# A message-passing layer on one core: index transfers spread over stage 1, one add for a group, sums of two groups in one bank, and 39 in place of 53 groups copied by hand

## The chip, the cores and the metric

The kernel runs on one core of one Trainium2 chip. The time is the device time of one execution in microseconds (us); a profile of one further execution gives what each engine did. TensorE is called PE (PEld is its loading of weights), VectorE DVE, ScalarE ACT, GpSimd POOL and SyncE SP in the profile.

## The reference, cut to what matters

There are 12,500 nodes with 128 features and 400,000 edges, sorted by their destination.

```
h   = relu(layernorm(x))
m   = relu(concat(h[src], h[dst], edge_attr) @ w1 + b1) @ w2 + b2
agg = segment_sum(m, dst)
out = x + GRU(agg, h)          # gates r, z, n from agg @ w_ih and h @ w_hh
```

As w1 has 288 rows, the first product splits into three: A = h @ w1[0:128] for the source, B = h @ w1[128:256] + b1 for the destination, and the edge part with the last 32 rows. The product with w2 is taken after the sum over edges.

## The kernel before

**Tiles, units, groups.** 128 edges make a tile, eight tiles (two halves of four) a group. There are 3,125 tiles and 391 groups, the first of them with five tiles. A half group is a unit `u`; the main loop (L1004) runs over 782 units. The order of the work on each engine is that of the program, written out by hand: what stands ahead in an engine's list must be done first.

**Stage 1** (L247 to L379) loops over 26 chunks of up to four tiles of 128 nodes. It loads x in batches of eight tiles (`load`, L263, five buffers), takes mean and variance on VectorE (`bn`, L187), normalises on ScalarE (`relu_norm`, L241), transposes on PE (L337) into `hT_all`, which keeps h transposed in SBUF, multiplies by the first part of w1 (L370), copies the result (`asb`, L346; three of four copies on VectorE) and stores it as table A in DRAM (L365). Ahead of the loop stand, on SyncE's queue, the loads of the first five batches, the weights, and 53 index rows `at` (L310 to L312), one for each group that is copied by hand. Behind the loop stand the stores of the statistics (L376) and the set-up of offsets and windows on VectorE (L398 to L496).

**Gathers.** `gather(k)` (L144) issues eight indirect DMAs on GpSimd for a group, each of 128 rows of A (or, for the first `RAW` = 10 groups, of x) into one of `GBUFS` = 12 tiles `G`. Rows of x are normalised and transposed again in the main loop (`raw_stats`, `raw_h`, `raw_turn`, L607 to L631).

**Groups by hand.** 53 groups are not gathered. For each, an engine copies 1,024 columns of `hT_all`, one edge at a time, at an address read into a register from `at` (`one_by_one`, L897): 26 groups on ScalarE (L909) and 27 on VectorE (L916, two edges at a time, and L921). PE multiplies these columns by the first part of w1 (L655). `SPREAD` (L55) gives the numbers, L90 to L98 spread the groups over the loop, and `run_jobs` (L937) cuts the copying into steps among the other work.

**The main loop.** `stages(u)` (L969) works ahead. `onehot_T` (L538) and `onehot` (L579) make the one-hot rows of the destinations within a window of 32 nodes. `pre(u)` (L636) multiplies one-hot rows and edge features (`L`) by a window of B and the edge part of w1 (`RW`, loaded by `window_rows`, L562) into a bank of PSUM. `add(u)` (L659) adds the gathered rows and takes the relu in one VectorE instruction (L668), for each unit, into one of four tiles `RB`; for a group by hand ScalarE takes the relu (L675). `seg(u)` (L679) sums the edges of a window with the one-hot matrix, one bank of PSUM for each group, which a product with zeros starts (L683). `take` (L692) copies a group's sums to SBUF. Every 14 groups make a block of up to 512 nodes, for which `node(b)` (L738) runs the GRU in steps spread over the next block's units; the last block has its own order (L802). Parts of B, 512 nodes each, are made in the main loop (`batch_product`, L216) at every 16th group, 32 groups ahead.

Of the kernel before, what the change touches and what calls it, by code (L numbers as in the profile page):

```python
# [11 lines left out]
I32 = mybir.dt.int32  # L12
# [23 lines left out]
BLOCKS = [(BP * b, BP, BW) for b in range(26)] + [(364, 10, 384), (374, 9, 352), (383, 8, 320)]  # L36
# [8 lines left out]
RAW = 10  # L45
GBUFS = 12
BATCH = 512
AHEAD = 32
ROOM = V * (AHEAD - 4)
# [5 lines left out]
SPREAD = {"dve": 27, "act": 26}  # L55
START = {"dve": 16, "act": 4}
# [6 lines left out]
def tile_gnn(ctx: ExitStack, tc: tile.TileContext, x, src, srcT, dstT, dstP, eaT, eaP, w1, b1, w2T, b2,  # L63
# [13 lines left out]
    wide = [ps1.tile([128, 512], F32, name=f"wide{i}") for i in range(2)]  # L77
# [35 lines left out]
    def dst_tile(c):  # L113
        if c >= NPL:
# [14 lines left out]
                   allow_small_or_imprecise_dtypes=True)  # L129
    A = dram.tile([N, D], F32, name="A")  # L130
# [29 lines left out]
    RB = [const.tile([128, GRP, D + 4], F32, name=f"RB{i}") for i in range(4)]  # L160
# [55 lines left out]
    def batch_product(j, pm, pool, name, bufs):  # L216
# [3 lines left out]
        rows = min(BATCH, N - n0)  # L220
        for i in range(0, rows, 128):
            m = min(128, rows - i)
            nc.tensor.matmul(pm[:m, i:i + D], hT_all[:, n0 + i:n0 + i + m], w1b, start=True, stop=True)
# [19 lines left out]


    st_all = const.tile([128, NT, 2], F32, name="st_all")
    nc.vector.memset(st_all[:, NFULL, :], 0.0)
    with tc.tile_pool(name="pp", bufs=3) as pp:  # L247
# [62 lines left out]
        for r in range(NJ):  # L310
            t0 = tiles(by_hand[r])[0]
            nc.sync.dma_start(at[r:r + 1, :], row(src[t0 * 128:(t0 + PAIR) * 128]))  # L312
# [13 lines left out]
        NC = len(chunks)  # L326
        for q in range(NC + 3):
# [5 lines left out]
            if 1 <= q <= NC:  # L333
                b, i0, c, e, P, n0 = chunk(q - 1)
                pts[q - 1] = wide[q % 2]
                for j in range(c, e):
                    nc.tensor.transpose(pts[q - 1][:, (j - c) * P:(j - c + 1) * P],  # L337
                                        xs[b][:P, j, :], ident[:P, :P])
                if e == bats[b][1]:
                    load(b + 5)  # L340
            if q >= 3:
# [3 lines left out]
                copy = nc.scalar.copy if q % 4 == 2 else nc.vector.tensor_copy  # L345
                copy(asb[b][:P, c:e, :], pas.pop(q - 3)[:P, :e - c, :])  # L346
# [11 lines left out]
            if q in (6, 8):  # L358
                batch_product(q // 2 - 3, ps1.tile([128, 512], F32, name="nd"), pp, "bt", 1)
            if q in (7, 9):  # L360
                batch_store(q // 2 - 3)
# [4 lines left out]
            if 2 <= q <= NC + 1:  # L366
                b, i0, c, e, P, n0 = chunk(q - 2)
                pas[q - 2] = ps2.tile([128, GRP, D], F32, name="pre")
                for j in range(c, e):
                    nc.tensor.matmul(pas[q - 2][:P, j - c, :], columns(b, j, j + 1)[:, 0, :],  # L370
                                     w1a, start=True, stop=True)
        for b0, b1, n in ((0, 1, BAT[0]), (1, 12, 8), (12, 13, BAT[12])):
            i0 = sum(BAT[:b0])
            for b in range(b0, b1):
# [5 lines left out]

    nc.vector.tensor_copy(wide[0][:, D:D + V], iota)
    p3 = ctx.enter_context(tc.tile_pool(name="p3", bufs=3, reuse_waits="tile"))
    TOT = p3.tile([128, 2 * BW - DMIN], F32, name="TOT", bufs=1)
    DEG = p3.tile([34, 2 * BW - DMIN], F32, name="DEG", bufs=1)
    nc.vector.memset(TOT, 0.0)
    nc.vector.memset(DEG, 0.0)
    nc.vector.memset(DEG[32:34, :BW], 1.0)


    dcol = p3.tile([128, BP + 128], F16, name="dcol", bufs=1)  # L390
    nc.vector.memset(dcol, 0.0)
    dlast = p3.tile([128, BLOCKS[-1][1] + 128], F16, name="dlast", bufs=1)
    nc.vector.memset(dlast, 0.0)
    sums = p3.tile([2 * V, BP, D + 1], F32, name="sums", bufs=1)


    base_f = const.tile([1, NP], F32, name="base_f")
    nc.vector.tensor_copy(base_f[:, 1:], base_d)  # L398
    nc.vector.memset(base_f[:, 0:1], 0.0)
    nc.vector.tensor_scalar(base_f, base_f, float(LAST), 0.0, op0=ALU.min, op1=ALU.max)  # L400
    nc.vector.tensor_copy(at_f[64:65, 512:512 + NP], base_f)
    nc.vector.tensor_tensor(at_f[64:65, :NP], at_f[64:65, 512:512 + NP], at_f[64:65, :NP], op=ALU.is_gt)
    nc.vector.tensor_reduce(beyond, at_f[64:65, :NP], AX.X, ALU.max)
    base_b = p3.tile([128, NP, 2], F32, name="base_b", bufs=1)
    pm = ps1.tile([128, 512], F32, name="misc")
    nc.tensor.matmul(pm[:, :NP], ones, base_f, start=True, stop=True)
    nc.vector.tensor_copy(base_b[:, :, 0], pm[:, :NP])
    nc.vector.tensor_scalar(base_b[:, :, 1], pm[:, :NP], float(SHIFT), None, op0=ALU.add)

    place_c = const.tile([2 * V, 1], F32, name="place_c")  # L410
    nc.gpsimd.iota(place_c, pattern=[[0, 1]], base=0, channel_multiplier=1,
                   allow_small_or_imprecise_dtypes=True)
    node_of = p3.tile([2 * V, NP], F32, name="node_of", bufs=1)
    for a in range(2):
        s = slice(V * a, V * (a + 1))
        nc.vector.tensor_scalar(node_of[s, :], base_b[s, :, a], place_c[s, :], float(-V * a),
                                op0=ALU.add, op1=ALU.add)
    blk_f = const.tile([1, NB], F32, name="blk_f")
    groups = [(0, NW, 0, BP, BW)] + [(b, b + 1) + BLOCKS[b] for b in range(NW, NB)]
    for b0, b1_, k0, n, w in groups:  # L420
        nc.vector.tensor_scalar(blk_f[:, b0:b1_], base_f[:, k0:k0 + (b1_ - b0 - 1) * n + 1:n], float(N - w),
                                None, op0=ALU.min)
    blk_i = const.tile([1, NB], I32, name="blk_i")
    nc.vector.tensor_copy(blk_i, blk_f)
    off_f = const.tile([1, NB, 16], F32, name="off_f")
    off_i = const.tile([1, NB, 16], I32, name="off_i")
    base_i = const.tile([1, NB, 16], I32, name="base_i")
    step_f = const.tile([1, NB], F32, name="step_f")
    step_i = const.tile([1, NB], I32, name="step_i")
    nc.vector.memset(off_f, 0.0)  # L430
    off_c = p3.tile([128, NB * 16], F32, name="gt", bufs=3)[:1, :].rearrange("o (b n) -> o b n", n=16)
    nc.vector.memset(off_c, 0.0)
    step_c = const.tile([1, NB], F32, name="step_c")
    nc.vector.tensor_tensor(step_f[:, 1:], blk_f[:, 1:], blk_f[:, :-1], op=ALU.subtract)
    nc.vector.memset(step_f[:, 0:1], float(BW))
    for b0, b1_, k0, n, w in groups:
        ks = base_f[:, k0:k0 + (b1_ - b0) * n].rearrange("o (b n) -> o b n", n=n)
        nc.vector.tensor_tensor(off_f[:, b0:b1_, :n], ks,
                                blk_f[:, b0:b1_, None].to_broadcast([1, b1_ - b0, n]), op=ALU.subtract)
        nc.vector.tensor_scalar(base_i[:, b0:b1_, :n], ks, float(4 * D), None, op0=ALU.mult)  # L440
        nc.vector.tensor_scalar(off_c[:, b0:b1_, :n], off_f[:, b0:b1_, :n], float(w - V - SHIFT), 0.0,
                                op0=ALU.min, op1=ALU.max)
    for b0, b1_ in [(0, 1), (1, NW + 1)] + [(b, b + 1) for b in range(NW + 1, NB)]:
        nc.vector.tensor_scalar(step_c[:, b0:b1_], step_f[:, b0:b1_], float(BLOCKS[max(b0 - 1, 0)][2]),
                                float(LEAST[b0]), op0=ALU.min, op1=ALU.max)
    nc.vector.tensor_copy(off_i, off_c)
    nc.vector.tensor_tensor(off_f, off_f, off_c, op=ALU.not_equal)
    nc.vector.tensor_copy(step_i, step_c)
    nc.vector.tensor_tensor(step_f, step_f, step_c, op=ALU.not_equal)
    dloc = const.tile([128, T], F16, name="dloc")  # L450
    lim = const.tile([128, 2, NPL], F32, name="lim")

    def place(c):
        if c >= NPL:
            return
        k0, k1 = c * PLACE, min(NP, (c + 1) * PLACE)
        t0, t1 = tiles(k0)[0], tiles(k1 - 1)[1]
        df = p2.tile([128, CH], F32, name="dst_f")
        nc.vector.tensor_copy(df[:, :t1 - t0], dst_i.pop(c)[:, :t1 - t0])
        if k0 == 0:  # L460
            for a in range(2):
                e = min(SUP0, (a + 1) * GRP)
                nc.vector.tensor_scalar(dloc[:, a * GRP:e], df[:, a * GRP:e],
                                        float(-SHIFT * a), None, op0=ALU.add)
        kb = max(k0, 1)
        tb = tiles(kb)[0]
        nc.vector.tensor_tensor(
            dloc[:, tb:t1].rearrange("p (k t) -> p k t", t=GRP),
            df[:, tb - t0:t1 - t0].rearrange("p (k t) -> p k t", t=GRP),
# [747 lines left out]
```

## Time and profile before

| | us |
|---|---|
| median of three runs | 3459.87 (3456.93 to 3460.8) |
| the profiled execution | 3466.03 |
| its span, first to last instruction | 3464.3 |

The page gives busy time by engine and by group of instructions. Rows of groups read: line, engine, operation, what is written and read, count, then busy time with the mean of one in ns, and behind the second bar the idle time of the engine just ahead of them and what ended most of it. Rows of the timeline read: start, duration, engine, line, operation, and in brackets the idle time before and what ended it ("issue" is time in which the engine waited for nothing that the profile shows). Rows of stretches give start and end, length, the busy time of PE, PEld, DVE, ACT and POOL with their instructions, the granted clock of PE, the busy share of the DMA engines and GB/s. The mean granted clock of PE was 0.796.

### The profile page before, as it was taken

What the parts mean: (1) busy time and instruction counts of PE and PEld (TensorE: products, weight loads), DVE (VectorE), ACT (ScalarE), POOL (GpSimd) and SP (SyncE); (2) the same over time, 40 slices, a digit from 0 to 9 for tenths busy, and PEclk for the clock granted to TensorE, in tenths of its full rate; (3) what the DMA queues carried; (4) which work ended last, traced back from release to release, by engine and by line L of the source; (5) the groups of instructions that cost most, each with busy time, mean ns of one, the idle gap of its engine ahead of it and who ended that gap; (6) DMA issues with size and microseconds to landing.
All of it is one profiled execution on the core that took longest, in us unless ns stands there. A gap on an engine that the chain in (4) does not pass through costs nothing. (4 is left out here: it accounts for less than half of the span.)

```text
span 3464.3 us, 83484 instructions
## 1 busy us (share of the span) xinstructions
PE 2463.0 (71%) x13272; PEld 1569.1 (45%) x13272; DVE 2298.2 (66%) x17007; ACT 2873.0 (83%) x27061; POOL 2596.0 (75%) x2710
## 2 busy tenths in 40 slices
PE   5567767767777776677767776776777667757767
PEld 5444444444444454454444444444444444434445
DVE  6756666666666676666666667666666666666673
ACT  4499798888879897979888889888988986998782
POOL 7577777777777777777777777777777777777776
PEclk8787787867877887777777778786888788888878
DMA  5433333333343333433333343333333433333332
GB/s 189 106 85 90 94 97 97 92 98 94 93 100 100 93 95 95 101 94 92 101 94 95 94 99 96 97 95 95 94 95 97 100 91 94 98 94 95 88 92 72
DMA packets 187723, 336.15 MB, mean 97 GB/s; under 512 B 64727, under 2 KB 108310, under 8 KB 187179
## 3 DMA queue, kind: packets, MB, share of 16 engines
q0 software_dynamic: 86432, 177.19, 21.9%
q1 hardware_dynamic: 100603, 153.54, 16.2%
q14 instruction: 434, 3.56, 0.3%
q8 instruction: 110, 1.80, 0.2%
q10 hardware_dynamic: 144, 0.07, 0.0%
HBM read 310.29 MB, written 20.26 MB: 95 GB/s over the span
## 5 line engine op out<-in xcount | busy, mean ns | idle before, releaser
L152 POOL DMA_INDIRECT G<-A,src_i x2624 | 2521.6, 961 | 826.7 <-issue 755.6
L909 ACT COPY HE_act<-hT_all 128x4 uint8 x26624 | 2683.1, 189 | 65.6 <-issue 42.2
L916 DVE SCALAR_TENSOR_TENSOR both<-hT_all 128x4 uint16 x13824 | 1181.6, 155 | 992.9 <-issue 983.2
L644 PE MATMUL pre<-RW,L 128*128 128x256 f32 x3128 | 1161.6, 499 | 878.1 <-DVE RB L668 839.3
L644 PEld LDWEIGHTS pre<-RW,L 128*128 128x128 f32 x3128 | 669.7, 239 | 1200.2 <-DVE RB L668 965.7
L688 PE MATMUL seg<-RB,OH 128*32 128x129 f32 x6250 | 614.2, 328 | 0.1
L668 DVE CUSTOM_DVE_ANT_0 RB<-pre,G 128x512 f32<-128x512 f32 x656 | 444.1, 677 | 43.4 <-DMA G<-A,src_i 20.2
L688 PEld LDWEIGHTS seg<-RB,OH 128*32 128x32 f32 x6250 | 335.8, 126 | 208.9 <-issue 151.8
L675 ACT ACTIVATE RB<-pre 128x512 f32<-128x512 f32 x126 | 74.3, 589 | 152.1 <-PE pre L655 151.8
L772 ACT ACTIVATE gt<-nd 128x512 f32<-128x512 f32 (+2 forms) x28 | 16.5, 588 | 219.6 <-PE nd L766 219.6
L545 DVE TENSOR_SCALAR L<-L,node_of 64x512 f32<-64x512 int32 x383 | 188.6, 493 | 5.9 <-DMA L<-in_dstP 5.9
L596 DVE TENSOR_TENSOR OH<-dloc,wide 128x256 f32<-128x256 f16 (+1 forms) x392 | 159.6, 407 | 0.5 <-issue 0.5
L713 PE MATMUL nd<-spot,sums 64*128 64x40 f32 x766 | 114.3, 319 | 0.0
L713 PEld LDWEIGHTS nd<-spot,sums 64*128 64x128 f32 x766 | 110.5, 229 | 7.7 <-issue 7.7
L683 PEld LDWEIGHTS <-zrow 1*64 1x64 bf16 x391 | 42.7, 109 | 156.7 <-issue 148.3
L696 DVE COPY sums<-seg 64x129 f32<-64x129 f32 x391 | 108.4, 277 | 3.8 <-PE seg L688 3.8
L683 PE MATMUL seg<-zrow 1*64 1x129 bf16 x391 | 104.1, 266 | 1.0 <-DVE sums L696 1.0
L921 DVE COPY HE_dve<-both 128x512 uint8<-128x512 uint8 x216 | 95.8, 443 | 7.4
L152 POOL DMA_INDIRECT G<-in_x,src_i x77 | 72.9, 946 | 24.5 <-issue 23.2
L655 PEld LDWEIGHTS pre<-w1a,HE_dve 128*128 128x128 f32 x432 | 80.0, 231 | 9.3
L655 PE MATMUL pre<-w1a,HE_dve 128*128 128x128 f32 x432 | 79.6, 316 | 0.0
L655 PEld LDWEIGHTS pre<-w1a,HE_act 128*128 128x128 f32 x416 | 72.1, 217 | 8.0
(193 smaller groups left out, 1395.5 us busy)
## 6 DMA issues: line engine op xcount, KB each, us to landing
L<-in_dstP SPq DMA_DIRECT2D x195, 256.0 KB
L<-in_eaP SPq DMA_DIRECT2D x195, 256.0 KB
G<-A,src_i POOLq DMA_INDIRECT x2624
RW<-B SPq DMA_DIRECT2D x782, 16.0 KB
xb<-in_x SPq DMA_DIRECT2D x26, 256.0 KB
out<-xb SPq DMA_DIRECT2D x26, 256.0 KB
xs<-in_x SPq DMA_DIRECT2D x11, 512.0 KB
A<-asb SPq DMA_DIRECT2D x11, 512.0 KB
```

The source lines that it names most:

```text
L152: nc.gpsimd.indirect_dma_start(out=G[k][:, j, a, :], out_offset=None, in_=table, in_offset=bass.IndirectOffsetOnAxis(ap=src_i[c][:, i:i + ...
L545: nc.vector.tensor_scalar(o, i, node_of[:, k:k + 1], None, op0=ALU.is_equal)
L596: nc.vector.tensor_tensor(o, d.to_broadcast(shape), i.to_broadcast(shape), op=ALU.is_equal)
L644: nc.tensor.matmul(PP[u][:, 2 * i:2 * i + 2, :], Ls[k // QP][:, c0:c0 + 128], RW[k % 4], start=True, stop=not raw)
L655: nc.tensor.matmul(PP[u][:, 2 * i + a, :], cols, w1a, start=False, stop=n + 1 == len(l) or l[n + 1][1] != j)
L668: nc.vector._custom_dve(TENSOR_ADD_SAT, out=RB[u % 4][:, :, :D], in0=PP.pop(u), in1=unit(u), s0=float("inf"), s1=0.0)
L683: nc.tensor.matmul(SEG[k][:2 * V, :D + 1], zrow[:, :2 * V], zrow[:, :D + 1], start=True, stop=False)
L688: nc.tensor.matmul(SEG[k][V * a:V * (a + 1), :D + 1], OH[k][:, j, a, :], RB[u % 4][:, (j % 2) * 2 + a, :D + 1], start=False, stop=all(b != ...
L696: nc.vector.tensor_copy(sums[:, slot(block(k), k - BLOCKS[block(k)][0]), :], pm[:2 * V, :D + 1])
L713: nc.tensor.matmul(p[:, bass.ds(offs[i], V + SHIFT)], sums[:, slot(b, i), :D], spot, start=False, stop=i == len(offs) - 1)
L909: nc.scalar.copy(he[:, e * 4:e * 4 + 4], column(v))
L916: nc.vector.scalar_tensor_tensor(both[:, (e0 % PIECE + i) // 2, :], column(vals[i + 1]), 256.0, column(vals[i]), op0=ALU.mult, op1=ALU.add)
```

## The change

- **Index transfers.** The rows `at`, now 39, are issued three to a chunk of stage 1, from the fifth step on.
- **Groups by hand.** `SPREAD` goes from 27 and 26 to 24 (VectorE) and 15 (ScalarE); with `RAW` = 9, nine groups are gathered from x.
- **One add for a group.** The product of a group's two units goes to one tile of two banks, and one add (or relu) covers it, into one of two `RB` tiles; only the last group's add is in halves.
- **Sums of two groups in one bank**, in different rows, taken by one copy after the second; `spot`, `dcol` and `sums` are laid out for it. The blocks at the end become 10, 8 and 9 groups.
- **Stage 1.** Every copy `asb` out of PSUM is on ScalarE; the set-up of offsets runs as a generator among the chunks; three parts of B in place of two are made there.
- **Later.** Parts of B are 448 nodes (14 windows of 32) and made in a block's node steps, three blocks ahead; constants are set at group 6 and the statistics stored at group 20.

```diff
-BLOCKS = [(BP * b, BP, BW) for b in range(26)] + [(364, 10, 384), (374, 9, 352), (383, 8, 320)]
+BLOCKS = [(BP * b, BP, BW) for b in range(26)] + [(364, 10, 384), (374, 8, 320), (382, 9, 320)]
-RAW = 10
+RAW = 9
-BATCH = 512
-AHEAD = 32
+BATCH = V * BP
+FIRST = 3
-SPREAD = {"dve": 27, "act": 26}
-START = {"dve": 16, "act": 4}
+SPREAD = {"dve": 24, "act": 15}
+START = {"dve": 14, "act": 4}
...
-        lo, hi = START[m] // 2 + 2, NP - {"dve": 9, "act": 6}[m]
+        lo, hi = START[m] // 2 + 2, NP - {"dve": 7, "act": 5}[m]
...
-        for r in range(NJ):
-            t0 = tiles(by_hand[r])[0]
-            nc.sync.dma_start(at[r:r + 1, :], row(src[t0 * 128:(t0 + PAIR) * 128]))
+        rows_left = list(range(NJ))
+
+        def at_row():
+            if rows_left:
+                r = rows_left.pop(0)
+                t0 = tiles(by_hand[r])[0]
+                nc.sync.dma_start(at[r:r + 1, :], row(src[t0 * 128:(t0 + PAIR) * 128]))
...
-                copy = nc.scalar.copy if q % 4 == 2 else nc.vector.tensor_copy
-                copy(asb[b][:P, c:e, :], pas.pop(q - 3)[:P, :e - c, :])
+                nc.scalar.copy(asb[b][:P, c:e, :], pas.pop(q - 3)[:P, :e - c, :])
...
+            if q >= 4:
+                for _ in range(3):
+                    at_row()
+            if q >= 6:
+                next(setting, None)
...
-        PP[u] = ps2.tile([128, GRP, D], F32, name="pre")
+        if h == 0:
+            PP[k] = ps2.tile([128, PAIR, D], F32, name="pre")
+        p = PP[k][:, GRP * h:GRP * h + GRP, :]
...
+        k, h = divmod(u, 2)
+        if h == 0 and k < NP - 1:
+            return
+        c = slice(0, PAIR) if k < NP - 1 else slice(GRP * h, GRP * h + GRP)
+        o, p = RB[k % 2][:, c, :D], PP[k][:, c, :]
...
-            nc.vector._custom_dve(TENSOR_ADD_SAT, out=RB[u % 4][:, :, :D], in0=PP.pop(u), in1=unit(u),
-                                  s0=float("inf"), s1=0.0)
+            nc.vector._custom_dve(TENSOR_ADD_SAT, out=o, in0=p,
+                                  in1=G[k].rearrange("p j a f -> p (j a) f")[:, c, :], s0=float("inf"), s1=0.0)
...
-        if h == 0:
-            SEG[k] = ps2.tile([128, 512], F32, name="seg")
-            nc.tensor.matmul(SEG[k][:2 * V, :D + 1], zrow[:, :2 * V], zrow[:, :D + 1],
-                             start=True, stop=False)
+        p = SEGB[(k // 2) % 2]
+        if h == 0 and k % 2 == 0:
+            nc.tensor.matmul(p[:, :D + 1], zrow[:, :128], zrow[:, :D + 1], start=True, stop=False)
...
-        if k < 0:
+        if k < 0 or (k % 2 == 0 and k < NP - 1):
             return
-        pm = SEG.pop(k)
-        nc.vector.tensor_copy(sums[:, slot(block(k), k - BLOCKS[block(k)][0]), :], pm[:2 * V, :D + 1])
+        b = block(k)
+        n = spots(k).stop
+        nc.vector.tensor_copy(sums[:n, slot(b, k - BLOCKS[b][0]), :], SEGB[(k // 2) % 2][:n, :D + 1])
...
-        yield 4 if b < NW else 1
+        yield 1
+        batch_product(b + FIRST, p3, "xb", 2)
+        yield 2 if b < NW else 1
         nc.sync.dma_start(out[bass.ds(g0, w), :].rearrange("(p i) f -> p i f", i=4), xb)
+        batch_store(b + FIRST)
...
+            if k == 6:
+                late_setup()
+            if k == 20:
+                store_stats()
```

More of the change, by code (lines that the diff above doesn't have):

```diff
@@ L76, in tile_gnn @@
     ps1 = ctx.enter_context(tc.tile_pool(name="ps1", bufs=1, space=bass.MemoryType.PSUM))
-    wide = [ps1.tile([128, 512], F32, name=f"wide{i}") for i in range(2)]
+    SEGB = [ps1.tile([128, 512], F32, name=f"seg{i}") for i in range(2)]
     dram = ctx.enter_context(tc.tile_pool(name="dram", bufs=1, space=bass.MemoryType.DRAM))
@@ L157, in tile_gnn @@
         gather(k)
-    RB = [const.tile([128, GRP, D + 4], F32, name=f"RB{i}") for i in range(4)]
+    RB = [const.tile([128, PAIR, D + 4], F32, name=f"RB{i}") for i in range(2)]
     for r in RB:
@@ L402, in tile_gnn @@
[L402 to L469, printed above, removed]
-            base_b[:, kb:k1, :].rearrange("p k a -> p (k a)")[:, :, None].to_broadcast(
-                [128, 2 * (k1 - kb), GRP]), op=ALU.subtract)
-        nc.vector.tensor_reduce(lim[:, 0, c:c + 1], dloc[:, t0:t1], AX.X, ALU.max)
-        nc.vector.tensor_reduce(lim[:, 1, c:c + 1], dloc[:, t0:t1], AX.X, ALU.min)
@@ L475, in tile_gnn @@
-    place(0)
-    dst_tile(1)
     w2ih = const.tile([128, 3 * D], F32, name="w2ih")
@@ L583, in onehot @@
         OH[k] = OHB[k % len(OHB)]
-        row = wide[0][:, D:D + V]
+        row = SEGB[((k - 3) // 2 + 1) % 2][:, 256:256 + V]
         for a in range(2) if k == 0 else (None,):
@@ L806, in last_node @@
         yield
-        pd = wide[1][:, :w]
+        pd = ps1.tile([128, 512], F32, name="misc")[:, :w]
         zero(pd)
@@ L815, in last_node @@
         h = hT_all[:, bass.ds(gv, w)]
-        pt = wide[0][:, :w]
+        pt = ps1.tile([128, 512], F32, name="nd")[:, :w]
         zero(pt)
-        for i in range(n - 4):
+        for i in range(n - 3):
             sum_of(b, pt, offs, i)
@@ L1024, in other @@
             run_jobs(u, phase)
-            if h == 0 and phase == 1 and batch_due(k):
-                batch_product(batch_due(k), wide[1], p3, "xb", 2)
-            if h == 1 and phase == 1 and batch_due(k):
-                batch_store(batch_due(k))
             if h == 0 and phase == 3:
```

209 lines of the change are left out of this document (148 added, 61 removed).

## The prediction

> **What bounds the kernel now.** I read the page's first and fifth parts, then the view of the gathers' own line, then GpSimd's timeline, because a busy share alone (ScalarE has the highest) doesn't say which engine is never late for a reason of its own.
>
> ```profile
> span 3464.3 us, 83484 instructions
> PE 2463.0 (71%) x13272; PEld 1569.1 (45%) x13272; DVE 2298.2 (66%) x17007; ACT 2873.0 (83%) x27061; POOL 2596.0 (75%) x2710
> L152 POOL DMA_INDIRECT G<-A,src_i x2624 | 2521.6, 961 | 826.7 <-issue 755.6
> L909 ACT COPY HE_act<-hT_all 128x4 uint8 x26624 | 2683.1, 189 | 65.6 <-issue 42.2
> L916 DVE SCALAR_TENSOR_TENSOR both<-hT_all 128x4 uint16 x13824 | 1181.6, 155 | 992.9 <-issue 983.2
> L668 DVE CUSTOM_DVE_ANT_0 RB<-pre,G 128x512 f32<-128x512 f32 x656 | 444.1, 677 | 43.4 <-DMA G<-A,src_i 20.2
> L696 DVE COPY sums<-seg 64x129 f32<-64x129 f32 x391 | 108.4, 277 | 3.8 <-PE seg L688 3.8
> L921 DVE COPY HE_dve<-both 128x512 uint8<-128x512 uint8 x216 | 95.8, 443 | 7.4
> L152 POOL DMA_INDIRECT G<-in_x,src_i x77 | 72.9, 946 | 24.5 <-issue 23.2
> ```
> ```profile
> L152 POOL DMA_INDIRECT G<-A,src_i x2624: 939/944/1700, 107.9 to 3447.0; - x188
> L152 POOL DMA_INDIRECT G<-in_x,src_i x77: 940/944/1099, 3.4 to 98.5; - x77
> ```
> ```profile
> 107.86 0.96 POOL L152 DMA_INDIRECT G<-A,src_i  x1 [8.26 <-DMA stats<-st_all]
> ...
> 134.37 0.94 POOL L152 DMA_INDIRECT G<-A,src_i  x1 [6.39 <-PE misc L629]
> ...
> 148.65 0.94 POOL L152 DMA_INDIRECT G<-A,src_i  x1 [4.56 <-PE misc L629]
> ...
> 242.66 0.94 POOL L152 DMA_INDIRECT G<-A,src_i  x1 [4.17 <-DVE RB L668]
> ...
> 327.13 0.94 POOL L152 DMA_INDIRECT G<-A,src_i  x1 [4.29 <-DVE RB L668]
> ...
> 3447.00 0.94 POOL L152 DMA_INDIRECT G<-A,src_i  x1 [0.30 <-issue]
> ```
>
> The two gather groups together: 2521.6 + 826.7 + 72.9 + 24.5 = 3445.7 us, busy and idle, for 2624 + 77 = 2701 gathers. That is the whole stretch from the first gather (3.4) to the end of the last (3447.94) and nearly the whole span. The 75% on the page is low only because each gather is followed by 0.30 us of "issue", in which it waits for nothing that the profile shows. The timeline holds just five waits that are longer: 8.26, 6.39, 4.56, 4.17 and 4.29, of which 27.67 - 5 x 0.30 = 26.2 us is real waiting. All five lie before 330 us. After that the gathers run without a hole to the end. So **GpSimd's gathers set the end**, at a pitch of (3445.7 - 26.2) / 2701 = 1.266 us, and what follows the last one, 3464.3 - 3447.9 = 16.4 us, is the tail. The chain of waits covers only the last microseconds and says nothing on this.
>
> The pitch seems to be the gather's own. The 77 gathers from x ran before any byte copy of ScalarE or VectorE, and their median is 944 ns, as it is for the 2624 beside the copies. Only the mean (961) is 17 ns above.
>
> **The change part by part.**
>
> *Groups moved back to gathers.* ScalarE's groups fall from 26 to 15 and VectorE's from 27 to 24, so 14 more of the 391 groups are gathered, eight gathers each: +112. The changed kernel's instruction list agrees: 69 + 2744 = 2813. At the pitch above this costs 112 x 1.266 = **+141.8 us**, all of it on the engine that sets the end. I see no work beside which it could lie.
>
> What it frees is off that path. ScalarE loses 11 x 2683.1 / 26 = 1135 us. VectorE loses, for each group, (1181.6 + 95.8) / 27 = 47.3 us of work and 983.2 / 27 = 36.4 us of waits ahead of it: 3 x 83.7 = 251 us.
>
> *One add for a group, sums of two groups in one bank.* VectorE: 656 adds of 0.677 us (444 us) become 342 twice as wide and two halves; bounded by no longer and twice as long, 233 to 464 us; I take 1.2 us each, nearer to twice, 412 us. Copies of sums fall from 391 to 196 of the same width for each partition: -54 us. PE drops 195 of the starting zero products. ScalarE's relus get wider and fewer. All of this lies beside the gathers and I cost it at nothing; if the cover were gone it would still be a gain. Only the later release could cost: a group's add now waits for its second half, so eight gather tiles come free together. With twelve groups of buffers that is half a group's delay of a 12-group store; I take 0 and bound it by one wait like those above, -0 to +4 us.
>
> *Index transfers.* Here is what the changed kernel wins.
>
> ```profile
> 20.08 17.73 SPq L312 DMA_DIRECT2D at<-in_src  x53
> 37.92 0.84 SPq L268 DMA_DIRECT2D xs<-in_x  x2
> 45.80 1.65 DVE L191 BATCH_NORM_STATS2 bn<-xs 128x6 f32<-128x128 f32 x8 [22.94 <-DMA xs<-in_x]
> 70.00:80.00 10.00, 9.48 (x48) 9.01 (x47) 9.73 (x50) 7.92 (x21) 7.56 (x9) 1.00 0.75 251
> 83.62 0.68 DVE L346 COPY asb<-pre 128x512 f32<-128x512 f32 x1
> 84.81 0.59 ACT L346 COPY asb<-pre 128x512 f32<-128x512 f32 x1 [2.51 <-PE pre L370]
> 105.33 0.29 DVE L346 COPY asb<-pre 84x128 f32<-84x128 f32 x1 [0.69 <-DMA A<-asb]
> 108.15 0.35 DVE L398 CAST base_f<-at 1x390 f32<-1x390 int32 x1
> 119.49 0.67 DVE L191 BATCH_NORM_STATS2 bn<-G 128x6 f32<-128x128 f32 x3
> 143.06 1.19 PE L644 MATMUL pre<-RW,L 128*128 128x256 f32 x2 [8.96 <-DMA RW<-B]
> ```
>
> SyncE issues 53 index rows in one go (0.33 us each) with the sixth load of x behind them at 37.92. It lands at 45.80, and all of stage 1 stands still for 22.94 us. With the rows three to a chunk, from the fifth chunk on, that load goes out at about 20 and lands some 4 to 8 us later, so about 20 of the 22.9 us go. What is late next is VectorE itself (9.73 of 10 us in the stretch from 70 to 80, the third of the busy times in its row; PE, the first, has 9.48). There the change takes 18 copies of A's chunks (0.68 us) off VectorE and puts them on ScalarE (0.59 us), and adds the set-up that now stands between 108.15 and 119.49: 12 against 11 us, nothing in sum. ScalarE goes from 7.9 of these 10 us to about 9.5 (some 3.7 chunks in 10 us, three quarters of them with 0.59 us more), so it nearly ties with the others and I add 2 us. A's last copy comes at 105.3 - 20 + 2 = 87 and is stored by about 90. With RAW at 9 the gathers from x, 69 of them, end at 3.4 + 69 x 1.266 = 90.8. The first gather from A then waits 0 to 3 us in place of 8.26.
>
> The next four waits are for buffers that the main loop frees late. It starts 18 us earlier by stage 1; on VectorE the 11 us of set-up go besides, and on SyncE, ahead of the loads of L, the stats stores (14 issues, estimated at 6 us by the 0.33 us of an index row and some waits). That makes 24 to 29 us, while the gathers come at most 8.0, 14.1, 18.3 and 22.2 us earlier at these four (the waits ahead of them, less 0.30 each, added up). So they lose their cause, the last by little. Taken together I leave 2 of the 26.2 us: **-24 us**; bounds -26 and 0.
>
> *Moved pieces.* Stats stores go to group 20 (some 6 us on SyncE, behind which window rows wait that are four groups, some 36 us, ahead), constants to group 6. Parts of B, now 448 nodes, are stored by the end of a block's node steps, at about group 14(b+2), and read from 14(b+3) - 4: ten groups, about 90 us, of slack. Nothing in sum. In the tail the last group's add is still in halves: 0, within 2 us either way.
>
> *Lighter VectorE.* Gathers next to some VectorE work are longer:
>
> ```profile
> 1514.58 0.94 POOL L152 DMA_INDIRECT G<-A,src_i  x1 [0.30 <-issue]
> 1515.38 0.67 DVE L792 TENSOR_TENSOR gt<-gt 128x512 f32<-128x512 f32 x1
> 1515.83 1.21 POOL L152 DMA_INDIRECT G<-A,src_i  x1 [0.30 <-issue]
> ```
>
> With 11% fewer hand copies there I take 1 ns off the pitch: 1.265. The floor is the median, 0.944 + 0.305 of gap = 1.249. The Trainium skill (SBUF — State Buffer, section Who interferes with whom) states that a VectorE tensor_tensor with both inputs in SBUF, or an op in a two-port mode, holds a port pair against GpSimd, while an op with at most one SBUF input outside these modes does not. The trace agrees on the pair above (both inputs in SBUF, 1.21 us against 0.94). By that rule the wider add, with one input in PSUM, does not slow the gathers, and the sum stays.
>
> **Sum**, on the profiled execution: 3.4 + 2813 x 1.265 + 2 + 16.4 = 3580.2, which is +116 on its span of 3464.3. That execution took 3466.03 with what lies around the span, 6.2 above the median of the three timed runs, 3459.87. I put the same difference on the median: **3576 us**, 3.4% slower.
>
> **The rivals.**
>
> 1. *The early waits stay.* If the sixth load still lands late (SyncE, in order, holding it for PE's transposes of the first batch), or the main loop still starts at about 120 because of the stores and the loads of L and RW (row at 143.06), the 24 us come back: 3600. Against it: the load stands ahead of the rows in the new order on SyncE.
>
> 2. *The gathers fall to their floor.* Only some gathers are longer than the median, and one beside L792 took 1.21 us. If the work that VectorE loses were just what stretches them, the pitch would go to 1.249: 3.4 + 3513.4 + 2 + 16.4 = 3535, on the median 3531; half of the way is 3553. Against it: L792 and the other block steps all remain, and of the hand copies 89%. The rule of the Trainium skill quoted above would allow this, as VectorE's hand copies read SBUF twice.
>
> 3. *The consumers become the bound.*
>
> ```profile
> DVE both L916 <- issue: 983.2, 875, 2.6
> ...
> 3449.68 0.69 DVE L668 CUSTOM_DVE_ANT_0 RB<-pre,G 128x512 f32<-128x512 f32 x1 [4.19 <-DMA G<-A,src_i]
> ```
> From the first product (143) to the last add (3449.7) a group took 8.46 us, with VectorE busy or waiting ahead of its hand copies 2298 + 983 = 3281 us. If the shared banks and the two group-wide result tiles chained PE and VectorE so that a group took over (3565 - 118) / 391 = 8.82 us, the gathers would wait for buffers; every 0.1 us above costs 39 us: at 9.0, 3650. Against it: VectorE gets some 337 us lighter (251 + 54 + 32), 0.86 us a group.
>
> 4. *Not slower.* The gather's base pitch itself holds contention from the byte copies on ScalarE, of which 42% go. The place is each gather. It decides at (3464.3 - 3.4 - 2 - 16.4) / 2813 = 1.223 us: 43 ns less for each gather means no change, and 50 ns less means 1.216, so 3442 on the span and 3438 on the median. Against it: the shortest of all gathers is 939 + 300 ns, and the 77 gathers that ran without any byte copies have the same median.
>
> **How the numbers follow.** Forecast (3565 to 3590) 73%; the early waits stay, in part or whole (3590 to 3602), 10%; floor of the pitch in part or whole (3529 to 3565) 8%; consumers (above 3602) 6%; not slower 3%. The range leaves out the consumers, the lower half of the pitch's way and the last rival: 3553 (half of the way to the floor) to 3602 (no early wait removed, 2 us of tail). A change below 0.2% couldn't be told from none by this kernel's measurement. Slower by more than that: 97%; within: 1%; faster: 2%.
>
> **What would show it.** In the changed profile: 2813 gathers at 1.26 to 1.27 us with no hole after 150 us; gathers as the longest wait of VectorE's add and PE's chain in the main loop, ScalarE's share near half; no wait of 20 us for x at stage 1's sixth batch, A's last copy at 84 to 92; the last gather at about 3564 and a tail of 16 us. It is wrong if gathers get shorter than 0.939 us, if GpSimd waits for VectorE's add again and again through the loop, or if stage 1 still ends after 100.

## The result, and the profile after

| | before | after |
|---|---|---|
| median of four runs, us | 3460.34 | 3579.10 |
| range of the runs | 3456.93 to 3464.28 | 3576.96 to 3579.47 |
| ratio (95% interval) | | 1.0341 (1.0328 to 1.0354) |
| profiled execution, us | 3466.03 | 3576.96 |
| its span | 3464.3 | 3575.2 |

The changed kernel is 3.4% slower, 3 us from the forecast of 3576. The page of its profile, the first lines and the groups that answer to those of before:

```profile
span 3575.2 us, 68446 instructions
...
PE 2457.1 (69%) x12857; PEld 1553.7 (43%) x12857; DVE 2118.9 (59%) x14920; ACT 1729.5 (48%) x15729; POOL 2693.8 (75%) x2822
...
L155 POOL DMA_INDIRECT G<-A,src_i x2744 | 2626.4, 957 | 838.1 <-issue 797.8
L947 DVE SCALAR_TENSOR_TENSOR both<-hT_all 128x4 uint16 x12288 | 1051.1, 152 | 1010.7 <-issue 1005.8
L940 ACT COPY HE_act<-hT_all 128x4 uint8 x15360 | 1542.8, 189 | 31.0 <-issue 17.5
...
L718 PE MATMUL seg<-RB,OH 128*32 128x129 f32 x6250 | 627.4, 334 | 632.3 <-DVE RB L695 626.5
...
L695 DVE CUSTOM_DVE_ANT_0 RB<-pre,G 128x1024 f32<-128x1024 f32 (+1 forms) x344 | 417.7, 1214 | 359.2 <-DMA G<-A,src_i 338.6
...
L803 ACT ACTIVATE gt<-nd 128x512 f32<-128x512 f32 (+2 forms) x28 | 16.5, 588 | 811.8 <-PE nd L797 811.8
...
L155 POOL DMA_INDIRECT G<-in_x,src_i x69 | 66.1, 958 | 21.8 <-issue 20.7
```

Every engine but GpSimd does less than before, and the kernel is slower. ScalarE fell from 83% to 48% and VectorE from 66% to 59%, while GpSimd's 2813 gathers took 2626.4 + 838.1 + 66.1 + 21.8 = 3552.4 us, busy and idle, of the 3575.2. The reader sees who is waiting in the last number of three rows: VectorE's add waited 338.6 us for gathers (20.2 before), PE's sums waited 626.5 us for such adds, and ScalarE 811.8 us for products of PE, whose list holds them behind such sums. GpSimd itself, from the timeline, together with the events of stage 1:

```profile
18.29 2.06 SPq L358 DMA_DIRECT2D xs<-in_x  x2
...
20.88 0.87 SPq L406 DMA_DIRECT2D at<-in_src  x3
...
22.57 1.65 DVE L194 BATCH_NORM_STATS2 bn<-xs 128x6 f32<-128x128 f32 x8 [0.89 <-DMA xs<-in_x]
...
89.29 0.26 ACT L441 COPY asb<-pre 84x128 f32<-84x128 f32 x1 [1.07 <-DMA A<-asb]
...
92.23 0.94 POOL L155 DMA_INDIRECT G<-A,src_i  x1 [2.16 <-DMA dst_i<-in_dstT]
...
3553.56 0.94 POOL L155 DMA_INDIRECT G<-A,src_i  x1 [0.30 <-issue]
```

The sixth load of x now goes out while the statistics of the fifth batch are still in work, the wait of 22.94 us for it is 0.89, A's last copy comes at 89.29 in place of 105.33, and the one wait of GpSimd over 0.45 us after its first gather is 2.16 us. From 92 us to 3554.5 there is no other.

### The profile page after: what moved, and what is told of

The parts are those of the page before. It is cut to its first block, busy times and chain, and to the rows that moved or that the text cites. A ratio compares the mean times of both kernels' runs of the same rounds, so it can differ in the third digit from the quotient of the medians.

```text
span 3575.2 us, 68446 instructions
## 1 busy us (share of the span) xinstructions
PE 2457.1 (69%) x12857; PEld 1553.7 (43%) x12857; DVE 2118.9 (59%) x14920; ACT 1729.5 (48%) x15729; POOL 2693.8 (75%) x2822
## 5 line engine op out<-in xcount | busy, mean ns | idle before, releaser
L155 POOL DMA_INDIRECT G<-A,src_i x2744 | 2626.4, 957 | 838.1 <-issue 797.8
L947 DVE SCALAR_TENSOR_TENSOR both<-hT_all 128x4 uint16 x12288 | 1051.1, 152 | 1010.7 <-issue 1005.8
L940 ACT COPY HE_act<-hT_all 128x4 uint8 x15360 | 1542.8, 189 | 31.0 <-issue 17.5
L718 PE MATMUL seg<-RB,OH 128*32 128x129 f32 x6250 | 627.4, 334 | 632.3 <-DVE RB L695 626.5
L695 DVE CUSTOM_DVE_ANT_0 RB<-pre,G 128x1024 f32<-128x1024 f32 (+1 forms) x344 | 417.7, 1214 | 359.2 <-DMA G<-A,src_i 338.6
L803 ACT ACTIVATE gt<-nd 128x512 f32<-128x512 f32 (+2 forms) x28 | 16.5, 588 | 811.8 <-PE nd L797 811.8
L704 ACT ACTIVATE RB<-pre 128x1024 f32<-128x1024 f32 x48 | 49.0, 1020 | 707.0 <-PE pre L678 675.7
L569 DVE TENSOR_SCALAR L<-L,node_of 64x512 f32<-64x512 int32 x382 | 187.5, 491 | 11.0 <-DMA L<-in_dstP 10.4
L713 PE MATMUL seg<-zrow 1*128 1x129 bf16 x196 | 45.0, 230 | 200.0 <-DVE OH L617 196.7
L617 DVE TENSOR_TENSOR OH<-dloc,seg 128x256 f32<-128x256 f16 (+1 forms) x392 | 160.1, 409 | 0.6 <-issue 0.5
L744 PE MATMUL nd<-spot,sums 128*128 128x40 f32 x782 | 132.1, 345 | 2.0 <-DVE sums L727 2.0
L744 PEld LDWEIGHTS nd<-spot,sums 128*128 128x128 f32 x782 | 127.3, 257 | 12.6 <-issue 10.2
L952 DVE COPY HE_dve<-both 128x512 uint8<-128x512 uint8 x192 | 87.0, 453 | 6.6
L155 POOL DMA_INDIRECT G<-in_x,src_i x69 | 66.1, 958 | 21.8 <-issue 20.7
L793 PE MATMUL misc<-DEG,brow 34*128 34x512 f32 (+2 forms) x112 | 69.2, 701 | 14.8 <-DVE gt L807 14.6
```

What stands on the lines that cost most here:

```text
L155: nc.gpsimd.indirect_dma_start(out=G[k][:, j, a, :], out_offset=None, in_=table, in_offset=bass.IndirectOffsetOnAxis(ap=src_i[c][:, i:i + ...
L569: nc.vector.tensor_scalar(o, i, node_of[:, k:k + 1], None, op0=ALU.is_equal)
L617: nc.vector.tensor_tensor(o, d.to_broadcast(shape), i.to_broadcast(shape), op=ALU.is_equal)
L695: nc.vector._custom_dve(TENSOR_ADD_SAT, out=o, in0=p, in1=G[k].rearrange("p j a f -> p (j a) f")[:, c, :], s0=float("inf"), s1=0.0)
L718: nc.tensor.matmul(p[r0:r0 + V, :D + 1], OH[k][:, j, a, :], RB[k % 2][:, 2 * j + a, :D + 1], start=False, stop=all(b != a for _, _, b in r ...
L744: nc.tensor.matmul(p[:, bass.ds(offs[i], V + SHIFT)], sums[:, slot(b, i), :D], spot[:, i % 2, :], start=False, stop=i == len(offs) - 1)
```

## The experiments

Eight kernels gave twelve runs. In four of these runs, on one chip, and in two more, on another, the engines stood waiting for "issue" ahead of their hand copies, and the kernel before took about 5400 us beside them; they can't be set against the others and are told together at the end of this section.

**The changed kernel with the old split.**

```diff
-SPREAD = {"dve": 24, "act": 15}
-START = {"dve": 14, "act": 4}
+SPREAD = {"dve": 27, "act": 26}
+START = {"dve": 16, "act": 4}
-        lo, hi = START[m] // 2 + 2, NP - {"dve": 7, "act": 5}[m]
+        lo, hi = START[m] // 2 + 2, NP - {"dve": 9, "act": 6}[m]
```

> The changed kernel with the split of before (27 and 26 groups by hand, 2701 gathers), the same kernel as new_form_old_split, whose runs and those of before beside it were all slowed by waits for instructions. Theory (the number of gathers sets the end): 3.3 + 2701 x 1.2655 + 2 + 18 = 3441 us where the kernel before has 3460, ratio 0.994. First rival (the new form of the loop costs time): 3460 or more, ratio 1.0 or more. Second rival (ScalarE and VectorE can't keep up): GpSimd waits for buffers in the loop, 3450 to 3470. If instructions come as slowly as in that run, ScalarE's and VectorE's copies set the time again, 5400 to 5500 us, and it tells nothing on these theories.

Measured: 3436.95 us, ratio 0.9937 (0.992 to 0.9953), the fastest of all. The page's rows of its gathers and the view of GpSimd's waits:

```profile
L155 POOL DMA_INDIRECT G<-A,src_i x2632 | 2520.9, 958 | 805.2 <-issue 762.6
...
L155 POOL DMA_INDIRECT G<-in_x,src_i x69 | 65.8, 953 | 21.9 <-issue 20.7
```
```profile
POOL G L155 <- issue: 783.3, 2570, 0.3
...
POOL G L155 <- DVE RB L695: 3.0, 10, 0.3
POOL G L155 <- DMA dst_i<-in_dstT: 3.3, 1, 3.3
```

The last gather ended at 3415.9. In the second view the last number is the longest single wait: none for VectorE's add is over the usual 0.3. With the split as it was, all other parts of the change together lose nothing; they win 22 us. What each of them wins alone was not run on these chips, but for the order of the rows (below). Against the changed kernel (3579.1) the 112 gathers make 142 us, or 140 by the two ratios, as the chips differ: 1.25 to 1.27 us each. The first rival (the form costs time) and the second (the copying engines hold it) fall.

**The old form with the new split.** The same three lines the other way, in the kernel before.

```diff
-SPREAD = {"dve": 27, "act": 26}
-START = {"dve": 16, "act": 4}
+SPREAD = {"dve": 24, "act": 15}
+START = {"dve": 14, "act": 4}
-        lo, hi = START[m] // 2 + 2, NP - {"dve": 9, "act": 6}[m]
+        lo, hi = START[m] // 2 + 2, NP - {"dve": 7, "act": 5}[m]
```

> The kernel before with 24 and 15 groups by hand (2813 gathers), the same kernel as old_form_new_split. Theory: 112 more gathers at 1.2655 us, the early waits of GpSimd stay: 3460 + 142 = 3602 us, 3595 to 3608, ratio 1.041. Rival (a good part of the change's loss comes from its new form): clearly under 3579, about 3520. If instructions come as slowly as in the first run, about 5190 us.

Measured: 3582.72 us, ratio 1.0356 (1.0338 to 1.0373). The rival falls, as the old form is no faster than the new one; with this split the two can't be told apart, as their intervals overlap (1.0338 to 1.0373 and 1.0328 to 1.0354). But the theory's number, 3595 to 3608, was missed by 12 us: the early waits did not stay. GpSimd's timeline has two of them:

```profile
123.92 0.94 POOL L152 DMA_INDIRECT G<-A,src_i  x1 [4.08 <-PE misc L629]
...
139.16 0.94 POOL L152 DMA_INDIRECT G<-A,src_i  x1 [5.53 <-PE misc L629]
```
```profile
17.66 13.32 SPq L312 DMA_DIRECT2D at<-in_src  x39
31.11 0.83 SPq L268 DMA_DIRECT2D xs<-in_x  x2
35.67 1.64 DVE L191 BATCH_NORM_STATS2 bn<-xs 128x6 f32<-128x128 f32 x8 [12.88 <-DMA xs<-in_x]
```

With 14 groups less by hand there are 14 index rows less in front of the sixth load; it goes out 6.8 us earlier and the wait for x falls from 22.94 to 12.88 us, with nothing but the split changed; the first wait for A goes, and the two later ones for VectorE's add (242 and 327 us) go as well. The long waits, less 0.30 each, come to 9 us in place of 26. The pitch without them falls as well, from 1.2655 to 1.2611 us, 12 us over the run. So the split itself takes away most of the waits that I had credited to the order of the rows.

**The rows in front again**, in the changed kernel, all issued ahead of stage 1's first batch:

```diff
+        for _ in range(NJ):
+            at_row()
         stat(0)
         sqr(0)
```

> The changed kernel with its 39 index rows issued in one go ahead of stage 1, the same kernel as rows_in_front. Theory (the rows hold the sixth load of x, and so stage 1 and the first gathers from A): VectorE waits some 10 to 15 us more for x, and GpSimd's long waits ahead of 150 us come to some 9 us, as in the old form with 39 rows, where they are 2 now: 3579 + 7 = 3586, 3583 to 3595. Rival (no part of the rows' order matters for the end): 3579, within 2.

Measured: 3594.27 us, ratio 1.0373 (1.0355 to 1.039), against 1.0341 for the changed kernel beside its own runs of before: 0.32%, 11 us. From the timeline:

```profile
18.05 12.45 SPq L406 DMA_DIRECT2D at<-in_src  x39
...
34.79 1.64 DVE L194 BATCH_NORM_STATS2 bn<-xs 128x6 f32<-128x128 f32 x8 [13.08 <-DMA xs<-in_x]
```
```profile
102.03 0.95 POOL L155 DMA_INDIRECT G<-A,src_i  x1 [12.47 <-DMA L<-in_dstP]
```

VectorE's wait of 13 us is back, and GpSimd's only long wait grows from 2.16 to 12.47 us. The mechanism is as forecast: rows, sixth load, stage 1, first gather from A. It is worth about 10 us with 39 rows: 10.3 us of wait in the trace, and 11 us by two ratios whose intervals barely part (1.0355 against 1.0354). Part of that wait is due to `RAW`: with nine groups from x the last of these gathers starts at 88.6 here, while with ten it starts at 98.3 in the old form with 39 rows, whose first gather from A, at 99.52, has no such wait.

**More by hand.** 28 groups on VectorE and 29 on ScalarE in the changed kernel.

```diff
-SPREAD = {"dve": 24, "act": 15}
+SPREAD = {"dve": 28, "act": 29}
```

> The changed kernel with 28 groups by hand on VectorE and 29 on ScalarE, 2669 gathers, the same kernel as more_by_hand. Theory: 32 gathers fewer than with 27 and 26 at 1.262 us: 3437 - 40 = 3397 us. Rival (the copying engines can't keep up: in the run with 27 and 26 VectorE waited only 110 us for gathers and ScalarE some 400 us in all, and four more groups need 84 and 309 us of them): 3410 or more, with long waits of GpSimd for VectorE's add.

Measured: 3467.27 us, ratio 1.0006 (0.9996 to 1.0015). The gathers ended at 3389.0. The theory's pitch puts that end at 3.3 + 2669 x 1.262 + 2 = 3373.6; they took 1.268 us each, 15 us more in all. The span, however, is 3466.1. Stretches around that point (PE, PEld, DVE, ACT and POOL busy):

```profile
3300.00:3350.00 50.00, 29.89 (x176) 20.66 (x174) 29.37 (x236) 45.08 (x440) 37.90 (x40) 0.71 0.39 96
3350.00:3390.00 40.00, 29.25 (x154) 17.15 (x155) 29.43 (x213) 36.01 (x347) 29.89 (x31) 0.84 0.36 85
3390.00:3420.00 30.00, 23.26 (x133) 16.55 (x131) 16.83 (x97) 25.31 (x242) 0.00 (x0) 0.77 0.19 53
```

GpSimd has nothing left after 3390, and hand copies go on to 3420 on ScalarE, which is busy for 92% of the whole span; the rest of the loop follows them. The rival was right on the outcome (over 3410) and wrong on the sign: GpSimd did not wait for buffers, as twelve of them let it run ahead to its end. At 57 groups by hand the copying engines are the bound, at 53 the gathers. Which of the two copying engines it is was not separated; ScalarE's 92% speaks for ScalarE.

**ScalarE's copies half as many again**, the same gathers; each second copy is written twice, the output is the same.

```diff
                     nc.scalar.copy(he[:, e * 4:e * 4 + 4], column(v))
+                    if i % 2:
+                        nc.scalar.copy(he[:, e * 4:e * 4 + 4], column(v))
```

> The changed kernel in which ScalarE does every second copy of its hand groups twice: 23040 in place of 15360, 770 us more work for ScalarE, the same 2813 gathers. Theory (a gather's pitch is its own, and ScalarE isn't on the path): 3579, within 4, pitch 1.262 us. Rival (ScalarE's copies lengthen the gathers, so the hand groups pay twice): with 11 groups' worth of copies put on, 43 ns for each gather, 3579 + 0.7 x 121 = 3660.

Measured: 4425.46 us, ratio 1.277. Neither number: the added load was far heavier than 770 us, as ScalarE's busy time rose by 1493 us (1729.5 to 3222.9). The page's groups, two rows of the view of waits (total, times, longest) and ScalarE's timeline:

```profile
L940 ACT COPY HE_act<-hT_all 128x4 uint8 x15360 | 2182.4, 189 | 849.0 <-issue 848.0
L155 POOL DMA_INDIRECT G<-A,src_i x2744 | 2627.1, 957 | 1568.5 <-issue 783.6
L942 ACT COPY HE_act<-hT_all 128x4 uint8 x7680 | 1484.8, 193 | 244.7
```
```profile
ACT HE_act L940 <- issue: 848.0, 936, 1.5
...
POOL G L155 <- DVE RB L695: 729.0, 73, 28.2
```
```profile
2000.19 0.29 ACT L940 COPY HE_act<-hT_all 128x4 uint8 x2 [0.91 <-issue]
2000.51 0.19 ACT L942 COPY HE_act<-hT_all 128x4 uint8 x1
2000.61 0.28 ACT L940 COPY HE_act<-hT_all 128x4 uint8 x2
2000.92 0.20 ACT L942 COPY HE_act<-hT_all 128x4 uint8 x1
2001.02 0.28 ACT L940 COPY HE_act<-hT_all 128x4 uint8 x2
```

Three copies take 0.41 us where three plain ones take 0.30, and 848 us of waits came with them. ScalarE, busy or waiting ahead of its copies for 4317 of the 4421 us, became the bound, and GpSimd waited 729 us for VectorE's add, so the time tells nothing on the rival. The gathers do: their mean, 957 ns, and the pitch without the long waits, 1.262 us, are those of the changed kernel. The rival had asked for 30 ns more (0.7 of its 43). But the longer run thins the copies out: 23,040 in 4421 us are 5.2 for each us, against 4.3 in the changed kernel, 21% more and not half.

The stronger evidence is the changed kernel with the old split, above: 26,624 copies in 3434.5 us, 7.8 for each us. From there to the changed kernel 42% of ScalarE's copies go, the step for which rival 4 of the prediction asked 43 ns, and the gathers' mean goes from 958 to 957 ns. So contention from ScalarE's copies that is worth anything near that is excluded.

**Four groups by hand on VectorE** in place of 24, in the changed kernel.

```diff
-SPREAD = {"dve": 24, "act": 15}
+SPREAD = {"dve": 4, "act": 15}
```

> The changed kernel with 4 groups by hand on VectorE in place of 24: 20 groups more are gathered, 2973 gathers. Theory with the pitch as it is: 3.3 + 2973 x 1.262 + 2 + 20.7 = 3778 us. With the part of the pitch above its median that comes from VectorE's hand copies gone (at most 13 ns): 3739. Which of the two shows how much of the pitch is VectorE's copies; on the theory that the gathers alone set the end it must lie between them.

Measured: 3772.5 us in one run. Its gathers' row:

```profile
L155 POOL DMA_INDIRECT G<-A,src_i x2904 | 2772.0, 955 | 887.8 <-issue 855.7
```

Its view by line, and the same two rows of the run with the rows in front, beside it on the same chip (the three numbers are the shortest, median and longest of one gather in ns):

```profile
L155 POOL DMA_INDIRECT G<-A,src_i x2904: 943/947/1717, 92.1 to 3748.7; - x194
```
```profile
L155 POOL DMA_INDIRECT G<-A,src_i x2744 | 2635.0, 960 | 849.0 <-issue 796.9
```
```profile
L155 POOL DMA_INDIRECT G<-A,src_i x2744: 943/947/1635, 102.0 to 3572.7; - x196
```

With five sixths of VectorE's copies gone the mean is 955, 5 ns less beside the same median, 947. The run with more ScalarE copies, on this chip too and with all of VectorE's copies, has a mean of 957, but its median is 944, so it lies 13 ns above its own median, as the rows in front do; here it is 8. The other runs go the same way: the mean lies 12 and 13 ns above the median with 24 groups on VectorE (the changed kernel and the old form with the new split), 14 and 17 with 27 (the new and the old form), 16 with 28. So about 5 of the 13 ns go with VectorE's copies; each figure is from one execution. VectorE is busy for 34% of this run and the time still follows the gathers' number.

**Runs on slow issue.** The first runs of the four kernels *new form with the old split*, *old form with the new split*, *rows in front* and *more by hand* had the kernel before at 5418 us beside them; two further kernels, on another chip, at 5397. These two are the kernel before with the rows spread over the first stage, and the changed kernel with 28 groups on each engine:

```diff
-        for r in range(NJ):
-            t0 = tiles(by_hand[r])[0]
-            nc.sync.dma_start(at[r:r + 1, :], row(src[t0 * 128:(t0 + PAIR) * 128]))
+        rows_left = list(range(NJ))
+
+        def at_row():
+            if rows_left:
+                r = rows_left.pop(0)
+                t0 = tiles(by_hand[r])[0]
+                nc.sync.dma_start(at[r:r + 1, :], row(src[t0 * 128:(t0 + PAIR) * 128]))
...
+            if q >= 4:
+                for _ in range(3):
+                    at_row()
```
```diff
-SPREAD = {"dve": 24, "act": 15}
+SPREAD = {"dve": 28, "act": 28}
```

The page's groups of the new form with the old split, on the first of the two chips:

```profile
L940 ACT COPY HE_act<-hT_all 128x4 uint8 x26624 | 2950.0, 190 | 2161.8 <-issue 2139.0
L155 POOL DMA_INDIRECT G<-A,src_i x2632 | 2516.1, 956 | 2800.6 <-DVE RB L695 1824.7
L947 DVE SCALAR_TENSOR_TENSOR both<-hT_all 128x4 uint16 x13824 | 1251.9, 155 | 1710.4 <-issue 1694.9
```

The work of each row is what it is elsewhere (189 against 190 ns for a copy, 956 for a gather); the waits ahead of the copies are 2139 us for ScalarE and 1695 for VectorE. Now GpSimd waits 1825 us for VectorE's add. (Some expectations speak of instructions that come slowly; the profile shows these waits as "issue" and no cause.) There a group by hand is dear and fewer of them win:

| kernel | groups by hand | us | ratio |
|---|---|---|---|
| rows in front, new form | 39 | 5131.8 | 0.947 |
| old form, new split | 39 | 5188.1 | 0.958 |
| new form, old split | 53 | 5510.4 | 1.014 |
| new form, 28 and 29 | 57 | 5707.9 | 1.052 |
| old form, rows spread (other chip) | 53 | 5408.6 | 1.002 |
| new form, 28 and 28 (other chip) | 56 | 5603.1 | 1.039 |

What had been expected of them:

> The changed kernel with the split of before: 27 groups by hand on VectorE, 26 on ScalarE, so 2701 gathers in place of 2813. Theory (the number of gathers sets the end): 3.3 + 2701 x 1.2655 + 2 + 18 = 3441 us, some 18 us under the kernel before, as the early waits of GpSimd are gone. First rival (the new form of the loop itself, one add for a group and two groups in one bank, costs time): 3460 or more. Second rival (ScalarE and VectorE can't keep up with gathers that no longer wait): GpSimd waits for buffers in the loop and the time is 3450 to 3470.

> The kernel before with 24 groups by hand on VectorE and 15 on ScalarE, nothing else changed: 2813 gathers. Theory: 112 more gathers at 1.2655 us, the early waits of GpSimd stay: 3460 + 142 = 3602 us, 3595 to 3608. First rival (a good part of the change's loss comes from its new form): clearly under 3579, about 3520.

> The changed kernel with its 39 index rows issued in one go ahead of stage 1, as before. Theory (the row transfers held the sixth load of x, and so stage 1 and the first gathers from A): VectorE waits some 15 us or more for x again, A is stored some 15 us later, GpSimd waits 8 us or more in all ahead of 150 us: 3587 to 3600 us. Rival (the rows were never what held it, or the earlier start of the main loop by the moved set-up covers it): 3579, no change.

> The changed kernel with 28 groups by hand on VectorE and 29 on ScalarE, so 334 groups and 2669 gathers. Theory: 3.3 + 2669 x 1.265 + 2 + 18 = 3400 us, if the copying engines keep up: ScalarE needs 29 x 103 = 2990 us for its copies and some 190 for the rest. Rival (they don't; a group by hand is late and holds PE and the adds, and GpSimd waits for buffers): over 3425, and the trace shows long waits of GpSimd for VectorE's add.

> The kernel before with one edit: its 53 index rows are issued three to a chunk of stage 1, from the fifth step on. Theory (the form of the changed kernel won its 22 us with the old split by the early waits of GpSimd, and the index rows are the main cause of these): VectorE's wait of 22.9 us for x goes, the first gather from A comes at about 93 in place of 108, and GpSimd's early waits fall from 26 us to 5 to 12, the rest staying as the set-up still stands between stage 1 and the loop: 3460 - 17 = 3443, 3438 to 3452, ratio 0.995. Rival (the moved set-up or the one add is what removed the waits): the waits only move to the next buffers, 3456 or more.

> The changed kernel with 28 groups by hand on each of ScalarE and VectorE, 2677 gathers; with 29 on ScalarE the gathers were done 77 us before the end and ScalarE's copies held the loop. Theory: one ScalarE group less frees some 105 us of ScalarE, which brings its end under that of the gathers: 3.3 + 2677 x 1.263 + 2 + 20 = 3406 us, 3400 to 3416, ratio 0.984. Rival (it is VectorE's 28 groups, or both, that held the loop): 3430 or more, with a tail of 40 us or more behind the last gather.

None of these expectations can be judged there. Left open are the two that ran only there: what the order of the rows alone is worth in the old form, and whether 28 and 28 beats 3437.

## Why the prediction was right, point by point

- **What bounds it.** Right. Four further kernels on the undisturbed chips, with 2701, 2813 and 2973 gathers, ended 16 to 21 us behind the last one. The list of long waits before missed one, 0.92 us at 3125.02, which is worth 0.6 us.
- **112 gathers, +141.8.** Right: 142 us (140 by the ratios) between two kernels that differ in the split alone. In the profiles it is 112 x 1.262 = 141.
- **The pitch.** I took 1.265 us; it is 3549.4 / 2813 = 1.2618 (from the first gather at 3.3 to the end of the last at 3554.5, less 1.9 us of long wait). Before it was 1.2655. It fell by 3.7 ns where I had taken 1, so the last gather ended at 3554.5 and not at about 3564, some 9 us on my good side. The old form with the new split has 1.2611 and the new form with the old split 1.2623, so either half of the change alone shows most of the fall. Lighter VectorE work fits, by the means above the medians (17 ns before, 12 after), but it isn't shown: single pitches scatter as much, and the rows in front, with the same copies on another chip, ran at 1.2649.
- **The rule on VectorE and GpSimd.** The Trainium skill (SBUF — State Buffer, section Who interferes with whom) states that a VectorE instruction with two SBUF inputs contends with a GpSimd instruction that reads SBUF, and lists ScalarE's ports as shared with no other engine; the prediction left out the words on reading. The trace of the changed kernel agrees. Gathers that ran for 0.3 us or more beside VectorE operations with two inputs in SBUF took 1171 ns (L823, 24 gathers), 1061 (L819, 25) and 958 (L617, 232) on average, and 946 beside the wider add L695 (442), which has one input in PSUM, as forecast; with no VectorE operation beside them for that long they took 950. But beside L569 and L952, with one SBUF input each, they took 984 and 981, and beside the add of the kernel before (L668) 972, which this part of the rule leaves open. On ScalarE's side, 42% fewer copies changed the mean by 1 ns.
- **The early waits, -24.** The size is right: 26.2 us became 1.9. The cause is right in part. The order of the rows gives about 10 us (the rows in front have 12.2 us of long waits), while the old form with 39 rows already has only 9 us. So with the rows still in front the other parts of the change (set-up and stores moved, `RAW` at 9, the new form) leave the sum of the waits no smaller; what the moved set-up and stores are worth, for which I had counted 11 and 6 us, can't be read from these runs. The step "with the rows three to a chunk, about 20 of the 22.9 us go" counted 53 rows, where the new split alone had taken 14 of them and 10 us with them.
- **The later release, moved pieces, stats stores: 0.** Right: GpSimd has no long wait after 92 us.
- **VectorE 337 us lighter (rival 3).** Too much, though off the path. 228 us of it was work, and VectorE's busy time fell by 179; the other 109 us were waits ahead of its hand copies, and these did not fall but rose by 23 (983.2 to 1005.8).
- **The tail, "0, within 2 us either way".** Failed: 20.7 us against 16.4. The two stretches behind the last gather, the kernel before first:

```profile
3448.00:3464.00 16.00, 7.89 (x39) 4.45 (x38) 5.00 (x12) 1.56 (x4) 0.00 (x0) 0.77 0.06 16
```
```profile
3554.50:3575.00 20.50, 8.64 (x26) 4.91 (x26) 4.96 (x11) 1.56 (x4) 0.00 (x1) 0.56 0.05 13
```

  VectorE and ScalarE do the same there; PE needs longer for fewer products at a granted clock of 0.56 against 0.77. Over these and three further profiles the tail goes with that clock: 15.8 us at 0.86 (old form, new split), 16.4 at 0.77, 18.6 at 0.68 (new form, old split), 20.7 at 0.56, 20.6 at 0.53 (rows in front). But the three with the longer tails are also the new forms, in which the sum of one group more waits for the last add, so clock and order are not told apart and the cause stays open.
- **From span to median.** I carried over the 6.2 us by which the profiled execution of before lay above its median. That of the changed kernel lies 2.1 below its own. The span was forecast at 3580.2 and is 3575.2, so two misses cancel in the 3 us.

The sum on the spans: +141.3 (gathers at the new pitch) - 10.0 (2701 x 3.7 ns) - 24.3 (early waits) + 4.3 (tail) = +111.3, measured +110.9.

## What to carry to other kernels

Where one engine issues back to back and all others keep ahead of it, the number of its instructions times their pitch is the time, whatever its busy share says: a change that lightens every other engine and adds 112 of its instructions is slower by these 141 us, less what it wins on that same engine (34 here, of waits and pitch). Read an engine's list of long waits before crediting a change with removing them, and ask of each part of the change alone what it takes away; here the smaller split alone had taken 10 us of the very wait for x that the new order was to remove. And on chips like those of the first runs the best split lies where the gathers' end and the copying engines' end meet: 53 groups by hand were gather-bound with 3437 us in the new form, 57 were copy-bound with 3467.

## What was not expected of the hardware

- The same kernel took 3460 us on some chips and about 5400 on two others, with unchanged durations of its instructions and "issue" waits of about 2000 us ahead of ScalarE's 26,624 small copies (42 us in the profile of before). GpSimd's gathers kept their length (956 ns). On the first of these chips the changed split is the faster one by 4 to 5% (ratios 0.958 in the old form, 0.947 in the new one with the rows in front; the changed kernel itself did not run there). What made issue slow there isn't shown.
- A repeated ScalarE copy to the place just written did not overlap with the one before: three copies took 0.41 us against 0.30 for three to different places, and 848 us of issue waits appeared in that run that the plain kernel doesn't have (17.5). They are 936 waits of some 0.9 us, about one for each of ScalarE's 960 loads of 16 addresses into registers (L934). Why the plain kernel does not wait there isn't shown.
